# Eleven ranks instead of thirteen with a block each, and eight experts' weights instead of seven fetched before the gate, in a fused GNN and mixture-of-experts kernel

## The chip, the cores and the metric

The kernel runs as one program on one core of a Trainium2 chip. The core has five engines that run side by side and meet only at semaphores: PE (TensorE, matrix products; its weight loads are shown as PEld), DVE (VectorE), ACT (ScalarE), POOL (GpSimd) and SP (SyncE). Sixteen DMA engines move data between the large memory (HBM) and the on-chip memory (SBUF); transfers are issued from the queues of SP, ACT and POOL. The metric is the time on the device in microseconds (us), as the median of several runs. Separately, one execution is recorded by the hardware profiler, and all the durations below come from that record.

## The reference: what is computed

Four layers act on x, which has 384 rows (graph nodes, called tokens below) of 512 floats. Each layer is a graph step over 6144 edges and then a feed-forward step, each on the normalized x and added back to it. Only the last feed-forward step (layer 3) bears on the change. It is a gated mixture of 64 experts:

```
scores = sigmoid(x2 @ gate_w.T)                       # 384 x 64
# best 4 of 8 groups of experts, then the best 8 experts of each token
h = silu(xb @ w1[e]) * (xb @ w3[e])                   # w1, w3: 512 x 256
y = (h @ w2[e]) * weight of the token for e           # w2: 256 x 512
```

Each token takes 8 of the 64 experts, so 384 x 8 = 3072 pairs of a token and an expert are computed. How many tokens an expert gets depends on the data. An expert's three matrices have 512 KB each, 1.5 MB together.

## The kernel before, in words

**Ranks and blocks.** The number of tokens of each expert is known only once the gate has been computed, late in the kernel. The experts are therefore given ranks. The experts 0 to `STATIC`-1 keep their own number as their rank (the kernel calls them static). The others get the ranks from `STATIC` on, in descending order of their token counts: lines 1358 to 1370 compare the counts of all pairs of experts (`first_row` and `first_col`, lines 243 to 248, add a large number to the static ones). Rank 0 is computed for all 384 tokens without a gather. The ranks 1 to `SINGLES`-1 have a block of 128 slots each. The remaining ranks go two to a block, 64 slots each. With `STATIC` = 7 and `SINGLES` = 14 there are 13 single blocks (ranks 1 to 13) and 25 pair blocks, 38 in all. `BLOCKS` (lines 48 to 53) is their order: ranks 1, 2, 3, then a few pair blocks after each further single, and the last single at the end. The order is written out when the program is built and doesn't depend on data.

**What is done for a block** (the loop of line 1672). POOL gathers up to 128 rows of the normalized x by an indirect DMA (`gather`, line 1505), four blocks ahead. PE turns the rows (`turned`), multiplies by w1 and w3 (`hidden`), turns the result (`turned_hidden`), and multiplies by w2 (`output`, line 1541). DVE scales by the token's weight, and POOL scatters the rows to a table `parts` in HBM. A slot without a token has a row number out of bounds, and such rows aren't moved. The last three blocks (`DIRECT`) are added into PSUM by a matmul with a selection matrix instead (`placed`). While they run, the table comes back from HBM in six transfers of 1 MB (`gathered_back`, line 1569) and is summed by DVE and PE.

**Where weights lie.** There are eleven places of 12 KB per partition, 8 KB for w1 and w3 and 4 KB for w2. Seven (`W_BUFS`) exist from the start and hold the weights of all earlier layers as a stream of turns. Four more (`MORE`) are opened after `layers.close()` at line 1336, in memory that the earlier layers used. Static experts can be fetched before the gate, since their number is known: ranks 0 to 4 come as the last entries of the weight stream (line 204), and 5 and 6 are fetched by hand at lines 1224 to 1227 and 1315 to 1316, into the two places that the graph step's weights `wn` and `ws` leave. All other experts are fetched once the ranks are known. Lines 1383 to 1394 work out at build time which place each gets: first the `MORE` places and that of rank 0, then the place of each block as it ends. `load(i)` at line 1395 issues those of w1 and w3 at the start of block i, and those of w2 one block later. All of them go through SP's queue in a fixed order (`issue_after`), and SP waits there until a place is free.

**Ranks with more tokens than slots.** `limit` (lines 1600 to 1603) holds the slots of each rank. `exceeded` (line 1614) counts the tokens of each rank, and `many` gets the largest value of 384 + count - slots. At the end every engine reads it and branches:

```
plain[1].memset(limit[:, 1:SINGLES], float(P))        # 128
plain[1].memset(limit[:, SINGLES:], float(HALF))      # 64
V.scalar_tensor_tensor(most, p, float(N), limit, op0=OP.add, op1=OP.subtract)
V.tensor_reduce(many, most, AX.X, OP.max)
count = nc.values_load(many[0:1, 0:1], min_val=0, max_val=2 * N)
with tc.If(count > N), ExitStack() as s4:             # N = 384
```

The body of this branch (lines 1744 to 1776) computes all 64 experts for all 384 tokens, in order of rank: for each it fetches the three matrices, makes 16 matmuls of 384 columns for the hidden values (`gate` and `value`, two halves, four steps each) and 6 of 512 columns for the output, and adds to x with a weight that is zero except for tokens beyond their rank's slots. At its end x is written out again. Its matmuls stand in the program expert by expert: those of the next expert come behind all six output matmuls of this one.

Of the kernel before, what the change touches and what calls it, by code (L numbers as in the profile page):

```python
# [8 lines left out]
F32 = mybir.dt.float32  # L9
# [7 lines left out]
P = 128  # L17
N = 384
NT = N // P
D = 512  # L20
KC = D // P
# [7 lines left out]
MAGIC = 12582912.0  # L29
NEG = -1.0e30  # L30
W_BUFS = 7
MORE = 4
STATIC = 7
SINGLES = 14
HALF = P // 2
FAR = 1.0e6
AHEAD = 4
# [9 lines left out]

_ones = [(r,) for r in range(1, SINGLES)]
_twos = [(r, r + 1) for r in range(SINGLES, 64, 2)]
BLOCKS, _ones, _left = _ones[:3], _ones[3:], _twos[:]  # L50
while _left:
    BLOCKS += _left[:2] + _ones[:1] + _left[2:3] * (len(_ones) < 8)
    _left, _ones = _left[2 + (len(_ones) < 8):], _ones[1:]

GROUPS = [[(r,) for r in c] for c in (range(1, 4), range(4, STATIC), range(STATIC, 11), range(11, SINGLES))]
GROUPS += [_twos[i:i + 5] for i in range(0, len(_twos), 5)]
# [37 lines left out]
def gnn_ffn_kernel(ctx: ExitStack, tc: tile.TileContext, a, out: bass.AP):  # L94
# [5 lines left out]
    turns_of_slots = [0]  # L100

    def slot(i=None):

        if i is None:
            i, turns_of_slots[0] = turns_of_slots[0] % W_BUFS, turns_of_slots[0] + 1
        return wpool.tile([P, 4 * D], F32, name=f"w8_{i}")
# [28 lines left out]
    def load_kn(src, k, n, queue=nc.sync):  # L135
        def load():
            w = slot()
            v = w.rearrange("p (k n) -> p k n", k=k)
            queue.dma_start(v, src.rearrange("(k p) n -> p k n", p=P))
            return v  # L140
        return load
# [8 lines left out]
            return w  # L150
        return load

    late, more, order = [], [], []

    RANKED = "a rank has one expert: the permutation's numbers are those of the experts"
    issued = []
# [1 line left out]
    def expert_of(order, r):  # L158
        return nc.values_load(order[0:1, r:r + 1], engines=[mybir.EngineType.SP], min_val=0, max_val=E3 - 1,
                              skip_runtime_bounds_check_because=RANKED)  # L160

    def load_expert(r, i):


        with tc.issue_after(issued[-1].ins) if issued else ExitStack():
            if i is None:
                i = slot_of[r] = turns_of_slots[0] % W_BUFS
                turns_of_slots[0] += 1
            e = r if r < STATIC else expert_of(order[0], r)
            w = (slot(i) if i < W_BUFS else more[0].tile([P, 4 * D], F32, name=f"w8_{i}")).rearrange(  # L170
                "p (i k n) -> p i k n", i=2, k=KC)
            for i_, n in enumerate(("L3_ffn_w1", "L3_ffn_w3")):
                how = "o (p k) n -> p (o k) n" if r else "o (k p) n -> p (o k) n"
                issued.append(nc.sync.dma_start(w[:, i_], a[n][bass.ds(e, 1)].rearrange(how, p=P)))
        experts_w[r] = [w, e]

    def load_second(r, i):

        with tc.issue_after(issued[-1].ins):
            w = (late if i < W_BUFS else more)[0].tile([P, 2, D], F32, name=f"w4_{i}")  # L180
            w, e = w, experts_w[r][1]
            issued.append(nc.sync.dma_start(w, a["L3_ffn_w2"][bass.ds(e, 1)].rearrange("o (p k) n -> p (o k) n", p=P)))
        experts_w[r][1] = w

    def load_static(r):
        def load():
            load_expert(r, None)
            load_second(r, slot_of[r])
        return load

    experts_w, slot_of = {}, {}
# [9 lines left out]
        + [load_kn(a["L2_gnn_WT"], KC, D)]  # L201
        + [load_pair(a["L2_ffn_w1"][e], a["L2_ffn_w2"][e]) for e in range(E2)]
        + [load_kn(a["L3_gnn_W_selfT"], KC, D), load_kn(a["L3_gnn_W_neighT"], KC, D)]
        + [load_static(r) for r in range(STATIC - 2)],
        W_BUFS)

    def row(name, n=D, pool=None):

        v = a[name]
        r = (pool or rows).tile([P, n], F32, name="row" if pool is None else "row_" + name)  # L210
        nc.scalar.dma_start(r, bass.AP(tensor=v.tensor, offset=v.offset, ap=[[0, P], [1, n]]))
        return r
# [30 lines left out]
    first_row = const.tile([64, 64], F32, name="first_row")  # L243
    V.tensor_scalar(first_row, nodes[:64, :64], -1.0, float(STATIC), op0=OP.mult, op1=OP.add)
    V.tensor_scalar(first_row, first_row, 0.0, 1000.0, op0=OP.max, op1=OP.mult)
    first_col = const.tile([64, 1], F32, name="first_col")
    V.tensor_scalar(first_col, lane[:64, :], -1.0, float(STATIC + 1), op0=OP.mult, op1=OP.add)
    V.tensor_scalar(first_col, first_col, 0.0, 1000.0, op0=OP.max, op1=OP.mult)
# [78 lines left out]
    with ExitStack() as s1:  # L327
# [68 lines left out]
        for t in range(NT):  # L396
            sb = ep.tile([P, EL], F32, name="gq", bufs=GQ_BUFS)
            for cs in halves:
                p = ps.tile([P, D], F32, name="mm")
# [7 lines left out]
        for t in range(NT):  # L407
            with tc.issue_after(shown.ins), tc.issue_after(ended.ins):
# [3 lines left out]
                for h, cs in enumerate(halves):  # L412
                    p = ps.tile([P, D], F32, name="mm")
# [16 lines left out]
        with tc.tile_pool(name="pa", bufs=1, space=bass.MemoryType.PSUM) as pa:  # L430
# [59 lines left out]
            for c in range(EC):  # L490
# [34 lines left out]
                for h in range(by_scalar(c)):  # L525
                    j = ep.tile([P, 2 * HD0], F32, name="junk", bufs=2)
# [42 lines left out]
    p = ps2.tile([P, NT], F32, name="acc")  # L569
# [388 lines left out]
    for i in range(3):  # L958
# [3 lines left out]
        if i > 0:  # L962
            w = stream.take()
# [13 lines left out]
        for f in range(KC):  # L977
            p = ps2.tile([P, N], F32, name="acc")
# [7 lines left out]
            j = qp.tile([P, N], F32, name="sq")  # L986
# [63 lines left out]
    for t in range(NT):  # L1050
        busy(8 if t == 0 else 3, pt.tile([P, D], F32, name="tp"))
        turn(qs[t], q1T, t, 2, BF16)
        p = ps2.tile([P, D], F32, name="acc")
# [6 lines left out]
    w = stream.take()  # L1060
# [8 lines left out]
    for t in range(NT):  # L1069
        p = ps.tile([P, D], F32, name="mm")  # L1070
# [11 lines left out]
    for t in range(NT):  # L1082
        p = ps2.tile([P, D], F32, name="acc")
        for s in range(NT):
            T.matmul(p, lhsT=A1[:, s, t * P:(t + 1) * P], rhs=g[:, s, :], start=s == 0, stop=s == NT - 1)
        r = sm.tile([P, D], F32, name="r512", bufs=2)
# [116 lines left out]


    ws, wn = stream.take(2)
    gamma, beta = row("L3_gnn_gamma"), row("L3_gnn_beta")
    b = row("L3_gnn_bias")
    xn, xT = rows_tile(), features()
# [7 lines left out]
    for t in range(NT):  # L1216
        p = ps.tile([P, D], F32, name="mm")
# [3 lines left out]
        evacuate(hn[:, t, :], p)  # L1221
        V.tensor_add(x[:, t, :], x[:, t, :], beta)

    slot_of[STATIC - 2] = (turns_of_slots[0] - STATIC + 2 - 1) % W_BUFS
    slot_of[STATIC - 1] = (turns_of_slots[0] - STATIC + 2 - 2) % W_BUFS
    load_expert(STATIC - 2, slot_of[STATIC - 2])
    load_second(STATIC - 2, slot_of[STATIC - 2])
    xnd = dram.tile([N, D], F32, name="xnd")
    gT = features("gT", pool=moe, bufs=1)
# [83 lines left out]
    to_experts(1, ps_[1])  # L1313
    ps_.append(convolved(2))
    load_expert(STATIC - 1, slot_of[STATIC - 1])
    load_second(STATIC - 1, slot_of[STATIC - 1])
    turn(rows_of[1], gT, 1)
    to_experts(2, ps_[2])
# [33 lines left out]
    p = pt.tile([P, NT, E3], F32, name="tp")  # L1352
# [22 lines left out]
    p = ps2.tile([1, E3], F32, name="acc")  # L1375
# [6 lines left out]

    free = [(-3, W_BUFS + i) for i in range(MORE)] + [(-2, slot_of[0])]
    where = {r: i for i, b in enumerate(BLOCKS) for r in b}
    free += [(where[r], slot_of[r]) for r in range(1, STATIC)]
    firsts, seconds = {}, []
    for b in BLOCKS:
        for r in b:
            if r >= STATIC:
                free.sort()  # L1390
                end, i = free.pop(0)
# [177 lines left out]
    def gathered_back(t):  # L1569

        halves_ = []
        for h in range(2):
            i = rooms.pop(0)
            r = (slot(i) if i < W_BUFS else more[0].tile([P, 4 * D], F32, name=f"w8_{i}")).rearrange(
                "p (j d) -> p j d", j=4)
            nc.sync.dma_start(r, view[t, :, 4 * h:4 * h + 4, :])
            halves_.append(r)
        back.append(halves_)
# [22 lines left out]
    plain[1].memset(limit[:, :1], float(N))  # L1601
    plain[1].memset(limit[:, 1:SINGLES], float(P))
    plain[1].memset(limit[:, SINGLES:], float(HALF))
    many = moe.tile([P, 1], I32, name="many", bufs=1)
# [67 lines left out]
    for i, b in enumerate(BLOCKS):  # L1672
# [48 lines left out]
        if i == len(BLOCKS) - DIRECT:  # L1721
            free.sort()
            rooms = [n for _, n in free]
            for t in range(NT):
                gathered_back(t)
# [17 lines left out]
    with tc.If(count > N), ExitStack() as s4:  # L1743
# [4 lines left out]
        for r in range(E3):  # L1748
            w = slot()
# [9 lines left out]
            for m in range(2):  # L1759
                c = slice(m * P, (m + 1) * P)  # L1760
                p = ps.tile([P, N], F32, name="mm")
# [3 lines left out]
                p = ps.tile([P, N], F32, name="mm")  # L1765
# [3 lines left out]
            for t in range(NT):  # L1769
                p = ps2.tile([P, D], F32, name="acc")  # L1770
# [39 lines left out]
```

## Time and profile before

| | |
|---|---|
| median of 3 runs | 831.5 us (830.15, 831.5, 835.92) |
| the profiled execution's own time | 846.38 us |
| its span, first to last instruction | 844.6 us |
| mean granted PE clock | 0.972 of full speed |
| busy: PE, PEld, DVE, ACT, POOL | 764.0, 356.3, 460.3, 275.3, 230.3 us |
| moved by DMA | 211.86 MB |

The profiled execution is longer than the runs by 14.9 us, and sums that are made in the profile are compared with its span. On the page, engines are followed by their busy share in 40 slices of the span, 21.1 us each. A busy PE isn't a PE at its peak: matmuls overlap, and a matmul that waits for data inside its pipeline counts as busy. "The chain that ended last" follows the work back from the last instruction, at each step to what released it. In a group of instructions, "out<-in" names the tiles, and L88 is the line of a helper that records the calls of many lines, so that groups of L88 are told apart by their tiles.

### The profile page before, as it was taken

How to read it: one execution, taken by the hardware profiler on the slowest of the kernel's cores; microseconds unless marked ns; L12 is line 12 of the kernel's file. 1: busy time of each engine (PE TensorE's matmuls, PEld its weight loads, DVE VectorE, ACT ScalarE, POOL GpSimd, SP SyncE). 2: the span in 40 equal slices, each digit the busy share in tenths (PEclk: the TensorE clock that was granted, in tenths of full speed). 3: DMA queues.
4: the chain of work that ended last, by engine and by line, in shares of the span. 5: the costliest groups of instructions: out<-in, count | busy, mean ns of one | idle time of the engine just before them, and what ended most of it. 6: DMA issues, size and time to landing. Idle time of an engine off the chain costs nothing.

```text
span 844.6 us, 10213 instructions
## 1 busy us (share of the span) xinstructions
PE 764.0 (90%) x3020; PEld 356.3 (42%) x3034; DVE 460.3 (54%) x1200; ACT 275.3 (33%) x1043; POOL 230.3 (27%) x228
## 2 busy tenths in 40 slices
PE   6999877867898878998899999989999999999996
PEld 3444333323344543454355544544444444433332
DVE  4575867768678966647642253756434242422226
ACT  1144655655674872334242010321111111101100
POOL 0046777777650021000000000013333332322100
PEclk9999989989999999998999999999999999999999
DMA  9987876777518801320191461379999999999985
GB/s 336 410 320 234 273 254 206 258 258 220 170 52 339 309 3 35 120 80 1 23 357 49 143 232 76 112 285 372 403 408 406 405 392 393 391 382 396 393 323 216
DMA packets 71198, 211.86 MB, mean 251 GB/s; under 512 B 11615, under 2 KB 16351, under 8 KB 70368
## 3 DMA queue, kind: packets, MB, share of 16 engines
q1 hardware_dynamic: 40592, 135.56, 42.0%
q0 software_dynamic: 19728, 57.97, 20.0%
q10 hardware_dynamic: 10816, 17.61, 5.8%
q8 instruction: 26, 0.43, 0.2%
q14 instruction: 36, 0.29, 0.1%
HBM read 188.46 MB, written 29.83 MB: 258 GB/s over the span
## 4 chain that ended last, share of the span: by engine, by line
PE 44%; DMA 27%; DVE 17%; ACT 5%; issue 3%; another core or an unknown queue 2%; POOL 0%; SPq 0%; DVEq 0%; ACTq 0%; POOLq 0%
DMA w<-in_L_ffn_w_dram 24%; PE mm L468 7%; PE mm L88 7%; PE acc L88 6%; PE mm L290 5%; PE mm L1115 4%; PE acc L1128 3%; PE mm L470 3%; PE tp L88 3%; PE mm L967 2%; ACT junk L527 2%; DVE mx L88 2%; DVE gp L514 2%; DVE relu L523 2%
## 5 line engine op out<-in xcount | busy, mean ns | idle before, releaser
L88 PE MATMUL mm<-w,xe 128*64 128x512 f32 (+1 forms) x504 | 145.9, 598 | 4.8 <-DMA w<-in_L_ffn_w_dram 4.8
L468 PE MATMUL mm<-w,osT 128*128 128x512 bf16 x365 | 95.9, 407 | 7.8 <-ACT osT L393 3.4
L88 ACT ACTIVATE hide<-mm 128x256 f32<-128x256 f32 x38 | 14.6, 385 | 212.2 <-PE mm L88 200.5
L88 POOL DMA_INDIRECT xg<-xnd,src x38 | 39.4, 1036 | 156.3 <-DVE ye L88 132.0
L88 POOL DMA_INDIRECT parts<-ye,dst x35 | 38.0, 1085 | 153.3 <-DVE ye L88 147.1
L88 PEld LDWEIGHTS mm<-w,xe 128*64 128x64 f32 (+1 forms) x504 | 47.8, 148 | 75.2 <-issue 69.2
L88 PE MATMUL acc<-w,hT 128*64 128x512 f32 (+1 forms) x244 | 75.1, 604 | 0.0
L443 POOL DMA_INDIRECT gq<-qd,dsti x48 | 55.9, 1164 | 67.3 <-DMA qd<-gq 41.8
L88 DVE TENSOR_TENSOR hide<-hide,mm 128x256 f32<-128x256 f32 x38 | 16.1, 424 | 100.8 <-ACT hide L88 100.8
L527 ACT ACTIVATE junk<-gp 128x128 f32<-128x128 f32 x186 | 55.3, 299 | 47.8 <-issue 34.9
L468 PEld LDWEIGHTS <-osT 128*128 128x128 bf16 x378 | 38.3, 103 | 66.3 <-issue 28.7
L88 DVE TENSOR_SCALAR ye<-acc,wts 128x512 f32<-128x512 f32 x35 | 26.3, 750 | 58.4 <-PE acc L88 58.4
L453 POOL DMA_INDIRECT mat<-w,kidx x48 | 51.5, 1074 | 23.1 <-issue 10.5
L527 ACT ACTIVATE junk<-relu 128x128 f32<-128x128 f32 x147 | 43.7, 300 | 25.6 <-DVE relu L523 8.1
L523 DVE SCALAR_TENSOR_TENSOR relu<-mm,wa_relu 128x512 f32<-128x512 f32 x42 | 28.4, 686 | 43.0 <-remote 12.3
L472 PE MATMUL pc<-od,os 128*128 128x384 bf16 x144 | 29.9, 336 | 22.5 <-DVE od L379 19.2
L470 PE MATMUL mm<-gq,ident 128*128 128x512 f32 x84 | 43.4, 598 | 0.1
L290 PE MATMUL mm<-w,xT 128*128 128x512 f32 x96 | 43.1, 607 | 0.0
L437 POOL DMA_INDIRECT gp<-pd,srci x27 | 32.8, 1213 | 18.7 <-DMA pd<-gp 7.3
L88 PEld LDWEIGHTS tp<-ident,xg 128*128 128x128 f32 x164 | 23.6, 203 | 30.3 <-issue 27.0
L527 ACT ACTIVATION_READ_ACCUMULATOR junk<-gp 128x1 f32 x186 | 35.1, 189 | 0.0
L88 PE MATMUL mm<-w,xT 128*128 128x512 f32 x72 | 32.6, 600 | 1.9 <-ACT xT L88 1.4
(383 smaller groups left out, 1249.6 us busy)
## 6 DMA issues: line engine op xcount, KB each, us to landing
w<-in_L_ffn_w_dram SPq DMA_DIRECT2D x204, 512.0 KB
mat<-y ACTq DMA_DIRECT2D x2, 4608.0 KB
m<-mat SPq DMA_DIRECT2D x12, 768.0 KB
parts<-xg POOLq DMA_DIRECT2D x1, 6144.0 KB
w<-parts SPq DMA_DIRECT2D x6, 1024.0 KB
w<-in_L_gnn_Ww_dram SPq DMA_DIRECT2D x4, 1024.0 KB
w<-in_L_gnn_W_dram ACTq DMA_DIRECT2D x2, 1024.0 KB
qd<-gq SPq DMA_DIRECT2D x3, 516.0 KB
```

The costliest lines, as they stand in the source:

```text
L88: self.last = getattr(self.engine, name)(*args, **kwargs)
L290: last = T.matmul(p, lhsT=xT[:, k, t * P:(t + 1) * P], rhs=w(k), start=start and k == 0, stop=stop and k == kc - 1)
L437: G.indirect_dma_start(out=gp, out_offset=None, in_=pd, in_offset=bass.IndirectOffsetOnAxis(ap=srci[:, c:c + 1], axis=0))
L443: G.indirect_dma_start(out=gq, out_offset=None, in_=qd, in_offset=bass.IndirectOffsetOnAxis(ap=dsti[:, c:c + 1], axis=0))
L453: return G.indirect_dma_start(out=mats[c % 2], out_offset=bass.IndirectOffsetOnAxis(ap=kidx[:, c:c + 1], axis=0), in_=sums.pop(c), in_offs ...
L468: T.matmul(z[h], lhsT=osT[:, t, :], rhs=split[t][:, i, cs], start=t == 0 and i == 0, stop=False)
L470: T.matmul(z[h], lhsT=ident, rhs=gq[:, cs], start=False, stop=True)
L472: counts.append(T.matmul(pc[t], lhsT=os_[:, t * P:(t + 1) * P], rhs=od, start=c == 0, stop=c == EC - 1))
L523: done = V.scalar_tensor_tensor(g3[:, c8, :], z[h].rearrange("p (h k) -> p h k", h=HH), 0.0, wide[:, c8, :], op0=OP.max, op1=OP.mult)
L527: summed = S.activation(j, g3[:, h, :], AF.Identity, accum_out=w8[:, h:h + 1])
L1115: T.matmul(p, lhsT=gate[:, k, c], rhs=xT[:, k, :], start=k == 0, stop=k == KC - 1)
L1128: last = T.matmul(p, lhsT=hid[:, m, t * P:(t + 1) * P], rhs=w2[:, m, :], start=m == 0, stop=m == 1)
```

## The change

Three constants change, the order of blocks is written anew, and one expert more is fetched early.

- `SINGLES` goes from 14 to 12: ranks 1 to 11 have a block of 128 slots, and ranks 12 to 63 share 26 pair blocks. There are 37 blocks. After the first three singles come groups of 2, 3, 3, 3, 3, 4, 4 and 4 pair blocks, each followed by a single.
- `STATIC` goes from 7 to 8: expert 7 is static as well, and its weights are fetched before the gate. Of the single blocks, ranks 1 to 7 are static, and 8 to 11 are the four experts with most tokens among 8 to 63.
- A place is moved: `MORE` goes from 4 to 3, and a new pool `extra` with one place is opened ahead of the layer-3 graph step. Expert 5 is fetched into it there. Experts 6 and 7 take the two places by hand that 5 and 6 had. A helper `room` finds a place's tile.

```diff
-MORE = 4
-STATIC = 7
-SINGLES = 14
+MORE = 3
+STATIC = 8
+STREAMED = 5
+SINGLES = 12
...
-while _left:
-    BLOCKS += _left[:2] + _ones[:1] + _left[2:3] * (len(_ones) < 8)
-    _left, _ones = _left[2 + (len(_ones) < 8):], _ones[1:]
+for _n in (2, 3, 3, 3, 3, 4, 4, 4):
+    BLOCKS += _left[:_n] + _ones[:1]
+    _left, _ones = _left[_n:], _ones[1:]
...
-    late, more, order = [], [], []
+    late, more, extra, order = [], [], [], []
+
+    def room(i):
+        if i < W_BUFS:
+            return slot(i)
+        return (more if i < W_BUFS + MORE else extra)[0].tile([P, 4 * D], F32, name=f"w8_{i}")
...
-        + [load_static(r) for r in range(STATIC - 2)],
+        + [load_static(r) for r in range(STREAMED)],
...
     ws, wn = stream.take(2)
+
+    extra.append(ctx.enter_context(tc.tile_pool(name="extra", bufs=1)))
+    slot_of[STREAMED] = W_BUFS + MORE
+    load_expert(STREAMED, slot_of[STREAMED])
+    load_second(STREAMED, slot_of[STREAMED])
...
-    slot_of[STATIC - 2] = (turns_of_slots[0] - STATIC + 2 - 1) % W_BUFS
-    slot_of[STATIC - 1] = (turns_of_slots[0] - STATIC + 2 - 2) % W_BUFS
+    slot_of[STATIC - 2] = (turns_of_slots[0] - STREAMED - 1) % W_BUFS
+    slot_of[STATIC - 1] = (turns_of_slots[0] - STREAMED - 2) % W_BUFS
```

The remaining lines of the diff put `room(i)`, or the choice between `late`, `more` and `extra`, in place of the choice between two pools in `load_expert`, `load_second` and `gathered_back`.

More of the change, by code (lines that the diff above doesn't have):

```diff
@@ L169, in load_expert @@
             e = r if r < STATIC else expert_of(order[0], r)
-            w = (slot(i) if i < W_BUFS else more[0].tile([P, 4 * D], F32, name=f"w8_{i}")).rearrange(
-                "p (i k n) -> p i k n", i=2, k=KC)
+            w = room(i).rearrange("p (i k n) -> p i k n", i=2, k=KC)
             for i_, n in enumerate(("L3_ffn_w1", "L3_ffn_w3")):
@@ L179, in load_second @@
         with tc.issue_after(issued[-1].ins):
-            w = (late if i < W_BUFS else more)[0].tile([P, 2, D], F32, name=f"w4_{i}")
+            w = (late if i < W_BUFS else more if i < W_BUFS + MORE else extra)[0].tile([P, 2, D], F32, name=f"w4_{i}")
             w, e = w, experts_w[r][1]
@@ L1573, in gathered_back @@
             i = rooms.pop(0)
-            r = (slot(i) if i < W_BUFS else more[0].tile([P, 4 * D], F32, name=f"w8_{i}")).rearrange(
-                "p (j d) -> p j d", j=4)
+            r = room(i).rearrange("p (j d) -> p j d", j=4)
             nc.sync.dma_start(r, view[t, :, 4 * h:4 * h + 4, :])
```

## The prediction

> **What bounds the kernel now.** I read the page's slices first, then the chain that ended last, then windows of the last stage.
>
> ```profile
> PE   6999877867898878998899999989999999999996
> PEclk9999989989999999998999999999999999999999
> DMA  9987876777518801320191461379999999999985
> ...
> DMA w<-in_L_ffn_w_dram 24%; PE mm L468 7%; PE mm L88 7%; PE acc L88 6%; PE mm L290 5%; PE mm L1115 4%; PE acc L1128 3%; PE mm L470 3%; PE tp L88 3%; PE mm L967 2%; ACT junk L527 2%; DVE mx L88 2%; DVE gp L514 2%; DVE relu L523 2%
> ```
>
> From slice 28 on, DMA stays at 9 or more, while it was idle in slices before. The chain agrees: its largest single item, 24% of the span (203 us), is the experts' weights. From 600 us it is one weight transfer after another up to 810 us. So the expert loop is bound by DMA, and block count, PE and POOL have slack there. The windows show its two ends:
>
> ```profile
> core 0: us, PE busy (x) PEld busy (x) DVE busy (x) ACT busy (x) POOL busy (x), PEclk, DMA share, GB/s
> 506.00:510.00 4.00, 4.00 (x14) 1.98 (x13) 0.94 (x2) 0.59 (x1) 0.00 (x0) 1.00 0.13 53
> 510.00:514.00 4.00, 4.00 (x11) 1.83 (x10) 0.00 (x0) 0.59 (x1) 0.00 (x0) 1.00 0.02 4
> ...
> 564.00:568.00 4.00, 4.00 (x14) 2.02 (x14) 2.43 (x5) 0.63 (x2) 0.00 (x0) 1.00 1.03 409
> ...
> 584.00:588.00 4.00, 4.00 (x34) 1.87 (x31) 1.24 (x8) 0.70 (x2) 2.76 (x3) 1.00 0.86 326
> ```
>
> Ahead of the gate (506 to 514) DMA does next to nothing. After it, it is full, except for a dip at 584 to 588 (share 0.86).
>
> **Part 1: eight experts instead of seven at the gate.** The eighth moves 1.57 MB out of the full stretch, worth 1.57 MB / 0.405 MB per us = 3.9 us. Its three transfers stand on SP's queue behind those of expert 4, which end at about 502.7 us; SP's next work is the load at 515.3, then the write of xnd at 527.0. Three issues take 1.25 us here (0.80 + 0.43), and the data fills 506 to 510, where DMA is idle. The place overlaps memory that the layer-2 hidden tiles leave at 498. Cost nothing; if that cover were gone, xnd's write could be late by those 3.9 us.
>
> But the places are still eleven, so one fewer is free when the ranks are known: 4 experts can be asked for at 552.7 us instead of 5. Before, 13 transfers of 0.52 MB (6.8 MB) are issued by about 564, and DMA moves some 4.9 MB of weights by 568.2, when block 0 frees a place: 1.9 MB in hand. After, 10 transfers (5.2 MB): 0.3 MB in hand. Blocks 1 to 3 free places at 573.7, 579.8 and 586.9, one expert (3.9 us of DMA) per 5.5 to 7 us, so DMA runs dry in each gap. From the end of block 3 the remainder is the same: before, 57 experts less 5 and 3 are left; after, 56 less 4 and 3: 49 both times. As before is already dry there (the 0.86), the gain is eaten. I take -1 us, between -4 (no drying) and +3 (later dry gaps by the new order).
>
> **Part 2: 37 blocks instead of 38, order.** A block costs POOL two issues of 1.0 us, PE some 5.5 us (places freed at 568.2 and 573.7). None is on the chain between 600 and 810. The rows gathered and scattered stay the same, since empty slots aren't moved. The tail is a pair, a pair and a single in both. Zero; bounds -2 and +2.
>
> **Part 3: ranks with 64 slots.** This needs the token counts. I worked the reference's gate out on the given inputs. Expert 0 has 69 tokens and experts 1 to 7 have 34, 54, 44, 63, 33, 60 and 35. Experts 8 to 63, in descending order, begin 78, 72, 66, 65, 65, 62, 62, 61. **Five of these are over 64.** Before, ranks 7 to 13 have 128 slots and rank 14 has 61 tokens: nothing exceeds. After, only ranks 8 to 11 (78, 72, 66, 65) have 128. Rank 12 has 65 tokens in 64 slots. Then `many` is 384 + 65 - 64 = 385, which is over 384, and the branch at the end is taken, for one token.
>
> That the chip's own gate gives the same counts can be seen in the trace. An indirect DMA of 128 rows is 64 packets for pairs of rows (4096 bytes: both moved; 2052: one; 8: none) and 16 of 4 bytes. Scatters and the gather behind them come as bursts of 160 packets. The burst with rank 11's scatter and the gather of ranks 62 and 63 has 58 packets of 4096 and 3 of 2052: 119 rows, and 65 + 29 + 25 = 119. The one with the scatter of ranks 44 and 45 and rank 11's gather has 73 and 2: 148 = 42 + 41 + 65. The running sum of rows agrees with the reference at the end of every burst, up to rank 12's last scatter with 62. So rank 11 of before, the fifth of those over 64, has 65 tokens on the chip, and the arithmetic ahead of the gate isn't changed.
>
> The body's cost: nearest is the layer-2 expert loop, which has the same two shapes of matmul.
>
> ```profile
> 470.29 5.32 PE L1115 MATMUL mm<-xT,w 128*128 128x384 f32 x16
> 475.45 5.31 PE L1128 MATMUL acc<-w,hid 128*128 128x512 f32 x12
> 480.60 5.32 PE L1115 MATMUL mm<-xT,w 128*128 128x384 f32 x16
> ```
>
> Start to start, 16 matmuls of 384 columns take 5.16 us (0.322 each) and 12 of 512 take 5.15 (0.429 each). An expert of the body has 16 of the first and 6 of the second: 5.16 + 2.57 = 7.73 us of PE. Layer 2 has its next experts' matmuls ahead of the outputs; the body doesn't, so PE waits once per expert for DVE's product of the last hidden half. The end of the chain shows such a handover:
>
> ```profile
> 829.40 1.73 PE mm L88 x4
> 831.13 0.02 issue
> 831.15 0.76 DVE ye L88
> 831.92 0.04 issue
> 831.96 7.15 PE acc L88 x16
> ```
>
> It costs 0.02 + the DVE operation + 0.04. The product of 384 columns lies between the 256 (0.42 us) and the 512 (0.72) of the rows, 0.56. A matmul of 384 ends 0.17 us after the next may start (0.489 mean against 0.322). So 0.17 + 0.02 + 0.56 + 0.04 = 0.79, less one output matmul (0.43) that needs only the first half: 0.36, and up to 0.19 more for a weight load (190 ns in the rows) that is the product itself. I take 0.45, between 0 and 0.9 (nothing overlaps). 64 x (7.73 + 0.45) = 524 us; bounds 495 and 552.
>
> Beside it: weights need 1.57 MB per 8.2 us, half of what the stretch moves; SP issues three transfers in some 2 to 4 us; DVE has 2 x 0.56 + 3 x 0.75 = 3.4 us per expert; ACT 2 x 0.49. All hidden. "DMA: Bandwidth & Descriptors" (Bandwidth) of the Trainium skill gives, for transfers issued from GpSimd, 138 GB/s at 64 KB and 341 at 1 MB; at a middle 240, an expert's 512 KB transfers would take 6.5 us, still under 8.2; the row says 409, 3.8 us. At the front, SP has to wait for the first place until DVE has added what came back (835.4 in this trace), so the first matrices land at about 839 to 841, and PE, done at 839.1, goes on at about 841: 2 us. The branch itself took 45 to 76 ns where engines weren't waiting. The end (last sum, output) is as before.
>
> One rule speaks against the 524. "TensorE: Matmul & The Clock Gate" (HAM oscillation) says that PE falls to half its clock once it idles over about 3.4 us. Were that to happen in every expert, 64 x 15.9 = 1018 us. But the body's gaps are under 1 us, and in the rows above the clock was 1.00 (windows above, and all slices from 20 on stand at 9). I take full speed, with one cold window (1.7 us) in the bounds.
>
> Sum in the profile: 844.6 - 1 + 2 + 524 = 1370 us. These parts are PE and DMA at their own rates, so against the median: 831.5 + 525 = 1356 us.
>
> **Rivals.**
> A. *The branch is taken and PE streams, with a short stop per expert*: 1356, from 1325 (no stop) to 1386 (0.9 each). 77%.
> B. *The branch is taken, but the body runs at another pace*: its fetches, SP's register loads, or a lower clock set it, 9 to 11 us per expert: 1409 to 1537. For: nothing of the body is in the trace; instructions of 64 unrolled experts must be fetched from memory too. Against: the slack above. 19%.
> C. *Not taken* (it doesn't end slower). Mechanism: one token of the 65 at rank 12 goes to another expert, because the change's gate rounds otherwise. It decides at 64. Then parts 1 and 2 alone are left: 831.5 - 1 = 830.5 (827 to 836). For: it takes a single token. Against: all row sums fit, and no arithmetic ahead of the gate is edited. 4%, of which 1 in 4 faster by over 1%.
>
> **Numbers.** The likeliest is A. Range 1325 to 1440: all of A and the lower part of B (up to 9.5 us), leaving out C and most of B, under 2 in 10. 1% is about what a measurement of this kernel can tell from no change. Slower 0.96, within 1% 0.03, faster 0.01.
>
> **What would show it.** After: COMPARE_BRANCH followed, on all engines but POOL, by work of the body (lines 1744 on, moved down by about 9), 1024 matmuls of 384 columns and 384 of 512 behind 840 us, PE with a gap of 0.3 to 0.6 us per expert, some 100 MB more moved, DMA share near half; DMA gaps at 570 to 587, and the loop's end within 3 us of before. Wrong if there is no such stage; if experts follow one another at over 9 us; or if the loop ends over 4 us earlier.

## The result, and the profile after

The changed kernel takes **1828.24 us** (median of 4 runs, 1825.79 to 1830.64), the kernel before 832.61 us (830.15 to 835.92): a ratio of **2.200, with an interval of 2.193 to 2.207**. It is 996 us longer. The prediction was 1356 us, with a range of 1325 to 1440. The direction and its cause were right. The size was not: the added time was put at some 525 us, about half.

The page of the kernel after, first the slices (40 of 45.7 us each), then the largest groups of instructions (line, engine, operation, tiles and shapes, count, then busy us and mean ns of one):

```profile
PE   8987887989999999999999999999999999999999
POOL 0677711000002332200000000000000000000000
PEclk9999999999999999999999999999999999999999
DMA  9778671214548999998333333332332223333200
...
PE acc L1781 18%; PE mm L1772 18%; PE mm L1776 18%; DMA w<-in_L_ffn_w_dram 8%; PE mm L89 5%; PE acc L89 4%; PE mm L473 3%; PE mm L295 2%; PE tp L89 2%; PE mm L1120 2%; PE acc L1133 2%; DMA mat<-w,kidx 1%; ACT junk L532 1%; PE mm L972 1%; PE mm L475 1%
...
L1776 PE MATMUL mm<-gT,w 128*128 128x384 f32 x1024 | 351.2, 486 | 0.0
L1772 PE MATMUL mm<-gT,w 128*128 128x384 f32 x1024 | 351.2, 486 | 0.0
L1781 PE MATMUL acc<-w,ohid 128*128 128x512 f32 x768 | 348.2, 601 | 0.2 <-DVE ohid L1777 0.2
```

From slice 18 on (counted from 0) there is a stage that the kernel before doesn't have. PE is full, POOL does nothing, and from slice 19 DMA is at 2 or 3 tenths instead of 9, until it ends before PE does. Three lines carry the stage, 1772, 1776 and 1781. They are the products with w1, w3 and w2 in the body of the branch, and more than half of the chain. So the branch was taken. The counts are the second thing to see: 2048 matmuls of 384 columns and 768 of 512, where the prediction announced 1024 and 384.

The stage begins when the last sum of the expert loop is done and lasts to the end of the span (pieces of the chain, start and length in us):

```profile
819.47 7.13 PE acc L89 x16
826.60 2.58 PE mm L1772 x8
829.18 2.58 PE mm L1776 x8
831.76 2.58 PE mm L1772 x8
834.34 2.58 PE mm L1776 x8
836.92 5.28 PE acc L1781 x12
842.20 2.58 PE mm L1772 x8
```

One expert runs from 826.60 to 842.20, 15.60 us. Of these, 4 x 2.58 = 10.32 us are the hidden products and 5.28 the output products. Sixty-four make 998 us. That is the whole way to PE's last matmul, which ends at 1825 us, and nothing is added at the front: 826.60 is also where the loop's last matmul ends.

### The profile page after: what moved, and what is told of

It reads as the page before. It is cut to its first block, busy times and chain, and to the rows that moved or that the text cites. A ratio compares the mean times of both kernels' runs of the same rounds, so it can differ in the third digit from the quotient of the medians.

```text
span 1828.9 us, 17482 instructions
## 1 busy us (share of the span) xinstructions
PE 1754.6 (96%) x5841; PEld 881.9 (48%) x5841; DVE 675.0 (37%) x1529; ACT 334.7 (18%) x1169; POOL 226.4 (12%) x226
## 2 busy tenths in 40 slices
DMA packets 156489, 313.70 MB, mean 172 GB/s; under 512 B 14579, under 2 KB 84851, under 8 KB 155632
## 4 chain that ended last, share of the span: by engine, by line
PE 77%; DMA 11%; DVE 7%; ACT 3%; issue 2%; POOL 0%; ACTq 0%; SPq 0%; DVEq 0%; POOLq 0%
PE acc L1781 18%; PE mm L1772 18%; PE mm L1776 18%; DMA w<-in_L_ffn_w_dram 8%; PE mm L89 5%; PE acc L89 4%; PE mm L473 3%; PE mm L295 2%; PE tp L89 2%; PE mm L1120 2%; PE acc L1133 2%; DMA mat<-w,kidx 1%; ACT junk L532 1%; PE mm L972 1%; PE mm L475 1%
## 5 line engine op out<-in xcount | busy, mean ns | idle before, releaser
L1776 PE MATMUL mm<-gT,w 128*128 128x384 f32 x1024 | 351.2, 486 | 0.0
L1772 PE MATMUL mm<-gT,w 128*128 128x384 f32 x1024 | 351.2, 486 | 0.0
L1781 PE MATMUL acc<-w,ohid 128*128 128x512 f32 x768 | 348.2, 601 | 0.2 <-DVE ohid L1777 0.2
L1777 DVE TENSOR_TENSOR ohid<-ohid,mm 128x384 f32<-128x384 f32 x128 | 71.0, 555 | 580.2 <-PE mm L1776 580.2
L1772 PEld LDWEIGHTS mm<-gT,w 128*128 128x128 f32 x1024 | 194.6, 190 | 149.3 <-issue 30.1
L1776 PEld LDWEIGHTS mm<-gT,w 128*128 128x128 f32 x1024 | 194.6, 190 | 135.7
L1773 ACT ACTIVATE ohid<-mm 128x384 f32<-128x384 f32 x128 | 62.9, 491 | 943.5 <-PE mm L1772 925.4
L1781 PEld LDWEIGHTS acc<-w,ohid 128*128 128x128 f32 x768 | 140.6, 190 | 183.7 <-issue 122.5
L1782 DVE SCALAR_TENSOR_TENSOR x<-acc,far,x 128x512 f32<-128x512 f32 x192 | 144.2, 751 | 201.6 <-PE acc L1781 201.6
```

The lines of the kernel that those rows point to most:

```text
L1772: T.matmul(p, lhsT=gate[:, k, c], rhs=xT[:, k, :], start=k == 0, stop=k == KC - 1)
L1773: S.activation(hid[:, m, :], p, AF.Silu)
L1776: T.matmul(p, lhsT=value[:, k, c], rhs=xT[:, k, :], start=k == 0, stop=k == KC - 1)
L1777: V.tensor_mul(hid[:, m, :], hid[:, m, :], p)
L1781: T.matmul(p, lhsT=hid[:, m, t * P:(t + 1) * P], rhs=w2[:, m, :], start=m == 0, stop=m == 1)
L1782: V.scalar_tensor_tensor(x[:, t, :], p, far[:, t, r:r + 1], x[:, t, :], op0=OP.mult, op1=OP.add)
```

## The experiments

Three theories stand against each other. Theory T: the branch is taken for one token, and its body, 64 experts at 15.6 us, is the whole loss; the prediction's 8.2 us was half because in the trace one f32 product of the code (one matmul call) is two PE instructions. Theory F: 8.2 us an expert was right, and some 470 us are a fixed price of entering the branch, such as fetching instructions. Theory L: part of the loss comes from the new order, the place moved or the extra fetch. Each ratio is taken against runs of the kernel before on the same chip, and the chips differ. Its median was 830.25 us for the branch alone, half of the body, the change without the branch and rank 7 moved; 830.48 for eight static experts alone and eleven single blocks alone; 845.36 for the wait removed, one place fewer and the other order; and 830.73 for the outputs put behind. So ratios are compared, and times only where the chip is the same or it is said.

### The branch alone, in the kernel before

```diff
-V.scalar_tensor_tensor(most, p, float(N), limit, op0=OP.add, op1=OP.subtract)
+V.scalar_tensor_tensor(most, p, float(N + P), limit, op0=OP.add, op1=OP.subtract)
```

> The kernel before, with 128 more added to the count that the branch compares: the branch is taken, though no rank has more tokens than slots (its body adds zeros, and the output is the same). Theory T (the body alone makes the difference, at 64 x 15.6 us, since every f32 product is two PE instructions): 832.6 + 996 = 1828, 1815 to 1840. Theory F (an expert of the body costs 8.2 us as predicted, and some 470 us are a fixed cost of entering the branch): also about 1828. Theory L (a part of the loss comes from the new order of blocks or the place moved): under 1800.

Measured: 1827.42 us, ratio 2.202 (2.194 to 2.210), against 2.200 for the changed kernel. With none of the change in it, the branch costs what the change costs. L falls as an account of the loss.

### Half of the body

```diff
-        for r in range(E3):
+        for r in range(E3 // 2):
             w = slot()
```

> The changed kernel with the body over ranks 0 to 31 only; rank 12, the only one with a token beyond its slots, is among them, so nothing is left out of the output. T: 1828 - 32 x 15.6 = 1329, 1320 to 1340. F: 1828 - 32 x 8.2 = 1566.

Measured: 1328.1 us, ratio 1.603 (1.596 to 1.610). The 32 experts left out were worth 1828.24 - 1328.1 = 500 us, 15.6 each, and the 32 kept cost 1328.1 - 830.25 = 498. The two halves are alike, so F's fixed price of 470 us falls; the intervals of the two ratios leave room for less than 20 us. The end of its chain has the same pieces as the full body's:

```profile
1301.84 2.58 PE mm L1772 x8
1304.42 2.58 PE mm L1776 x8
1307.00 2.58 PE mm L1772 x8
1309.58 2.58 PE mm L1776 x8
1312.16 5.29 PE acc L1781 x12
1317.45 0.02 issue
1317.47 0.75 DVE x L1782
```

### The stop between an expert's hidden and output products

The prediction gave 0.45 us per expert to a stop of PE for DVE. In the kernel after it shows as a wait of a weight load (PEld) inside the output products (start, length, and in brackets the wait before and what ended it):

```profile
1212.30 0.30 PEld L1781 LDWEIGHTS acc<-w,ohid 128*128 128x128 f32 x2 [0.69 <-DVE ohid L1777]
```

Here the output products of an expert stand behind the next expert's hidden products:

```diff
+            behind.append((r, hid, w2))
+            if r:
+                put(*behind.pop(0))
+        put(*behind.pop(0))
```

(`put` holds the output products and the sum, unedited, and the branch is taken as in the first experiment.)

> The kernel before with the branch taken, as in the run of that kind before, but an expert's output products stand behind the next expert's hidden products, so that PE has no stop for DVE. If PE's stop is what is left beside streaming (15.59 measured per expert less 15.46): 64 x 0.13 = 8 us shorter, 1819 where the run with the stop has 1827. If the stop is the 0.45 of the prediction and the products stream faster than I read: 29 us shorter, 1798.

Measured: 1818.13 us (1813.48 to 1818.72), 9.3 us below the 1827.42 of the run with the stop, or 0.15 us per expert. The two ran on different chips, and their ratios (2.185 with 2.172 to 2.198, and 2.202) differ by 14 us with some 13 either way, so the size comes from the traces. The output products' busy time falls from 348.2 us, the same in both kernels with the stop, to 339.9, which is 8.3 us or 0.13 per expert, and DVE's share of the waits before their weight loads from 44.3 us to 0.2. In the timeline of PE (start, length, instructions) an expert is now streaming and nothing else:

```profile
1201.85 2.74 PE L1776 MATMUL mm<-gT,w 128*128 128x384 f32 x8
1204.43 2.74 PE L1772 MATMUL mm<-gT,w 128*128 128x384 f32 x8
1207.01 2.74 PE L1776 MATMUL mm<-gT,w 128*128 128x384 f32 x8
1209.59 5.31 PE L1754 MATMUL acc<-w,ohid 128*128 128x512 f32 x12
1214.74 2.74 PE L1772 MATMUL mm<-gT,w 128*128 128x384 f32 x8
1217.32 2.74 PE L1776 MATMUL mm<-gT,w 128*128 128x384 f32 x8
```

From 1201.85 to 1217.32 are 15.47 us, against 15.60 above, with the output group at 5.15 (1209.59 to 1214.74) instead of 5.28. The stop was 0.13 us, as the busy times say too.

### The change without the branch

```diff
-    plain[1].memset(limit[:, SINGLES:], float(HALF))
+    plain[1].memset(limit[:, SINGLES:], float(HALF + 1))
```

The token beyond rank 12's 64 slots is then left without that one expert's contribution; everything else is computed.

> The changed kernel with the limit of the ranks from 12 on set to 65 instead of 64: the branch isn't taken. Left out: the contribution of one expert to the one token beyond its slots. T: what is left is the rest of the change, the loop 2 us longer as in the two profiles: 832 to 837. Part 1 of the prediction: 831.6. L: over 850.

Measured: 831.1 us, ratio 1.0020 (0.9999 to 1.0041). A limit one higher takes the 996 us away: rank 12 had exactly one token too many, as the reference and the packets of the gathers said. Everything else in the change comes to 3.4 us at most, by the interval.

### A wait that the prediction did not see

The trace of after has a stop of PE early in the loop. Three of the rows of DVE there (in brackets: idle time before, and what ended it):

```profile
563.96 1.49 DVE L89 TENSOR_TENSOR sel<-slots,place 128x384 bf16<-128x384 f32 x3
567.14 0.56 DVE L89 TENSOR_TENSOR sel<-slots,place 128x384 bf16<-128x384 f32 x1 [1.70 <-PE mm L89]
571.18 0.54 DVE L89 TENSOR_TENSOR hide<-hide,mm 128x256 f32<-128x256 f32 x1
```

and behind them, in PE's rows:

```profile
571.87 0.48 PE L89 MATMUL tp<-ident,hide 128*128 128x128 f32 x2 [2.05 <-DVE hide L89]
```

With `STATIC` = 8, the second group of blocks (`range(4, STATIC)` in `GROUPS`) has four ranks, and its selection matrices (`sel`, which pick a block's tokens) have three buffers. The fourth waits for PE to read the first. Queued behind it on DVE is the product that block 2 needs (`hide`), so PE stood idle for 2.05 us. To take the wait away, rank 7 goes to the third group, which has five buffers; the limit is 65 again, with the same contribution left out:

```diff
-(range(1, 4), range(4, STATIC), range(STATIC, 11), range(11, SINGLES))
+(range(1, 4), range(4, 7), range(7, 11), range(11, SINGLES))
```

> As the one before (limit 65, one token's contribution of one expert left out), and rank 7 is moved from the second group of blocks to the third, so that the second has three selection matrices for its three buffers. If DVE's wait for a buffer (1.7 us, PE behind it 2.6) sets the start of the loop, this is 2 to 3 us shorter than the run with limit 65: 830 to 834. If DMA makes up for it later: no difference.

Measured: 827.47 us, ratio 0.9969 (0.9951 to 0.9988), 3.6 us less than with the wait (831.1, on the same chip). Windows of 4 us behind block 2, here of the run with the wait, then without (busy us of PE, PEld, DVE, ACT, POOL, then clock, DMA share, GB/s):

```profile
566.60:570.60 4.00, 2.89 (x14) 1.23 (x16) 2.99 (x13) 0.00 (x0) 1.79 (x2) 1.00 0.59 233
570.60:574.60 4.00, 4.00 (x31) 2.08 (x27) 0.42 (x1) 0.97 (x2) 1.25 (x2) 1.00 0.54 154
```

```profile
567.40:571.40 4.00, 4.00 (x35) 1.77 (x31) 1.33 (x8) 0.60 (x2) 2.85 (x3) 1.00 0.77 287
571.40:575.40 4.00, 4.00 (x18) 1.73 (x18) 1.82 (x8) 0.37 (x1) 1.02 (x1) 1.00 0.99 311
```

PE's hole is gone, and DMA, which takes its work from the places that blocks free, stands idle less.

### Eight static experts alone, and with the wait removed

Both are the changed kernel with thirteen single blocks and the order of before (the lines of the order aren't shown). The second also has rank 7 in the third group, with the edit above; nothing is left out.

```diff
-SINGLES = 12
+SINGLES = 14
```

> The change's eight static experts and moved place, with thirteen single blocks and the order of before (ranks 8 to 13 have 128 slots, none exceeds). If the place that is missing at the gate eats the saved fetch, as predicted, with the new wait for a selection buffer on top: 832 to 836. If the saved fetch counts in full: 828 to 829.

> Eight static experts with thirteen single blocks and the order of before, and rank 7 moved to the third group, so that no selection matrix waits for a buffer; nothing left out. If that wait cost 3 to 4 us in the run with eight static alone: 828 to 830. If the wait is not what made that run 2 us slower than before: 832.

Measured: ratio 1.0034 (1.0013 to 1.0055) with the wait, and 1.0003 (0.9984 to 1.0022) without. Without the wait, the eighth expert fetched ahead brings nothing beyond the interval. The difference of the two ratios, 0.0031 with some 0.003 either way, was taken across two chips; on one chip the wait's removal was worth 0.0051 (1.0020 against 0.9969). Both point to the wait as what made the first of the two slower.

### One place fewer

```diff
-MORE = 4
+MORE = 3
```

in the kernel before, and nothing else:

> The kernel before with three places opened at the gate instead of four, ten in all; the same experts fetched in the same order. If the place that is missing at the gate eats the saved fetch, a missing place alone costs about what a fetch saves: 2 to 5 us longer, 833 to 836. If the early gaps of DMA are hidden: no difference.

Measured: 850.05 us against 845.36, ratio 1.0063 (1.0038 to 1.0088): 5.3 us for the missing place, with 3.2 to 7.4 as its interval. An expert fetched ahead saves 3.9 us of DMA time, by the prediction's working; no run has that saving alone. That the two cancel fits the run with eight static experts and no wait, and isn't shown beyond that.

### Eleven single blocks alone, and another order

```diff
-SINGLES = 14
+SINGLES = 12
```

in the kernel before, with the order of blocks of the change (not shown) and seven static experts:

> The kernel before with seven static experts, and the change's eleven single blocks and order. Ranks 7 to 11 then have the five experts with over 64 tokens, and rank 12 has 62: the branch isn't taken. If blocks are off the path, as predicted: 830 to 835. If a block less counts on PE: 827. If the branch were taken by the eleven single blocks alone: 1828.

Measured: 829.65 us, ratio 0.9991 (0.9964 to 1.0019). No difference, and no branch. This is the half of the change that is harmless on these inputs: the singles are then ranks 1 to 6 and the *five* fullest of the experts 7 to 63. It takes both halves to leave the fifth expert over 64 in half a block. The order by itself, in the changed kernel with thirteen singles, eight static experts and rank 7 in the third group (only the lines of the order are shown):

```diff
-for _n in (2, 3, 3, 3, 3, 4, 4, 4):
+for _n in (2, 3, 3, 3, 3, 3, 2, 2, 2, 2):
     BLOCKS += _left[:_n] + _ones[:1]
     _left, _ones = _left[_n:], _ones[1:]
```

> As the run with thirteen single blocks and rank 7 in the third group, but with the pair blocks in groups of 2, 3, 3, 3, 3, 3, 2, 2, 2, 2 behind the singles. If the order has no part: equal to that run within 1 us.

Measured: ratio 0.9991 (0.9970 to 1.0012), against 1.0003 with the order of before. No difference. The one run that was faster than the kernel before (0.9969) leaves a contribution out, and of those that compute everything none was faster beyond its interval. Its lead over 1.0003, on another chip, was not separated into the block less, the new order and the chips.

## Why the prediction was right or wrong, point by point

**The branch (part 3).** Right. Rank 12 has 65 tokens, `many` reaches 385, and the branch decides the result. That no rank has more than one token too many is shown by the limit of 65; that rank 12 alone has one rests on the reference's counts and the packets. That the body alone is the loss is shown by taking the branch in the kernel before. Rival C, that the gate rounds otherwise, falls with the stage in the trace.

**The body's streaming time.** This is the step that failed: "16 matmuls of 384 columns take 5.16 us ... An expert of the body has 16 of the first and 6 of the second: 5.16 + 2.57 = 7.73 us". The durations per instruction were right; they are the same 2.58 us for 8 and 5.15 for 12 in the body. The counts were of two different things. The 16 and 12 in the rows of layer 2 are instructions; the 16 and 6 of the body are calls in the code. An expert of layer 2 has 8 calls of 384 columns and 6 of 512, and its rows show 16 and 12. The prediction read these rows as if each were a call, which would make them two experts; they are one. With two instructions per f32 call an expert of the body has 32 x 0.322 + 12 x 0.429 = 15.46 us. With this one count mended, the prediction's sum is 64 x 15.46 = 989 us for streaming, and with the measured stop 64 x 15.60 = 998. The trace of before was enough to see it: layer 2 has six experts, so 48 and 36 calls, and the trace has 96 rows of line 1115 with 384 columns and 72 of line 1128.

**The stop.** Predicted 0.45 us, measured 0.13 in the traces (0.15 by the times of the run without it, across two chips). It is the same misreading: what the first output product covers is two instructions, 0.86 us, and not 0.43. The handover itself was sized well, at 0.79 with DVE's product at 0.56: in the rows that product took 0.56 us, and the weight load behind it starts 0.88 us after the output products (1211.42 to 1212.30). What is left of the handover and of that weight load is the 0.13 us.

**What lies beside it.** Fetches, DVE, ACT and SP were hidden, as said. The stage over 200 us (columns as in the windows above):

```profile
1000.00:1200.00 200.00, 200.00 (x566) 106.24 (x565) 42.64 (x64) 12.77 (x26) 0.00 (x0) 1.00 0.31 102
```

DMA runs at 102 GB/s, so neither the 409 GB/s of the prediction nor its middle of 240, an estimate between two cited figures, was asked for. The clock stays at 1.00, with stops of 0.13 us. The rule that the prediction weighed, from "TensorE: Matmul & The Clock Gate" (HAM oscillation) of the Trainium skill, has PE slow down after idle times over some 3.4 us, and no stop here comes near that, so the stage agrees with it without being a test. That the 1018 us of this rule lie near the measured 998 is chance: the rows give twice as many instructions, at full speed.

**Front of the body.** Predicted 2 us, measured none: SP issued the first fetch at 812.0, 14.6 us ahead of the end of PE's last matmul of the loop, while DVE's sums went on to 827.3; it didn't wait for the last of them.

**Rival B** was nearer, but at 9 to 11 us per expert too low as well, and for reasons that the rows exclude: PE streams at a clock of 1.00 with stops of 0.13 us, so neither fetches nor register loads nor the clock set the pace. The two instruction queues of the page moved 1.11 MB, against 0.72 before.

**The prediction's signs.** The stage came, with 101.8 MB more moved (313.70 against 211.86), and the loop ended 2 us later once the traces are laid over each other at the gate (826.60 + 14.6 = 841.2 against 839.1), within the 3 us named. The counts, the gap and the DMA share did not come as said. Experts follow one another at 15.60 us, over the 9 us at which the prediction called itself wrong.

**Part 1, the eighth expert.** Its fetch went where the prediction put it: SP issued it at 488.2 us, right behind that of expert 4, and DMA, at 0.13 and 0.02 in this place before, was full for it (windows of the kernel after, whose times here are some 14.6 us earlier than in the trace of before):

```profile
492.00:496.00 4.00, 4.00 (x14) 2.02 (x13) 0.69 (x1) 0.59 (x1) 0.00 (x0) 1.00 1.00 404
496.00:500.00 4.00, 4.00 (x10) 1.71 (x9) 0.00 (x0) 0.59 (x1) 0.00 (x0) 1.00 0.08 29
```

-1 us was forecast, with the gain eaten by the missing place. Right in kind: 1.0003 without the new wait, and a missing place alone costs 5.3 us. That wait, of a fourth selection matrix for three buffers, was not in the prediction. It cost about 3 to 4 us, and DMA ran short behind it: 154 GB/s at 570.60 to 574.60 in the windows above, against 311 without it.

**Part 2, blocks and order.** Zero was forecast: 0.9991 (0.9964 to 1.0019) for eleven singles alone.

## What to carry to other kernels

Before a static shape is cut to the data, count the data against it, and see whether the fallback is exercised: here one token among 3072 pairs turned on a path that costs more than the whole kernel, and neither of the two edits alone would have. When rows of a trace are used to price code, first tie their counts to the calls of the code in the same stage, by one iteration whose calls are known. A prefetch that is paid for with a buffer taken from later may gain nothing where the later stage is fed as buffers come free; here it gained nothing that could be measured.

## What the runs showed of the hardware

An f32 matmul call is two PE instructions here, each as long as the columns ask (0.322 us for 384, 0.429 for 512), so a call costs 0.645 and 0.859 us: 1024 and 384 calls stood as 2048 and 768 rows. In the trace of before nine bf16 instructions of 512 columns take 1.94 us (line 468 at 56.43), 0.216 each. An f32 instruction of that width is twice as long, and an f32 call costs four bf16 instructions. PE at full load for about 1000 us kept its clock at 1.00. Entering a branch of 64 unrolled experts left no gap on PE: its first matmul of the body follows at the end of the loop's last, at 826.60. Its sequencer had reached the branch at 823.3, so a delay of up to 3.3 us could have been hidden there.
